# A graph network's edge MLP on one core: the layer-1 bias, a node-row split and an update bias change engines

## The chip, the core and the metric

The kernel runs on one core of one Trainium2 chip. The core has five engines, each with a queue of its own that is worked off strictly in order: TensorE (PE, with its weight loads shown apart as PEld), VectorE (DVE), ScalarE (ACT), GpSimd (POOL) and SyncE (SP, which here issues all the DMAs of the steady part). [...]The metric is the device time of the whole kernel in microseconds (us), lower is better.

## What is computed

128 graphs of 64 nodes with 128 channels. Every pair (i, j) of a graph goes through a two-hidden-layer MLP, the messages are masked by the adjacency and summed over j, and a second MLP updates the nodes:

```
def _mlp(x, w0, b0, g0, be0, w1, b1, g1, be1, w2, b2):
    h = relu(x @ w0 + b0);  h = _layernorm(h, g0, be0)
    h = relu(h @ w1 + b1);  h = _layernorm(h, g1, be1)
    return h @ w2 + b2

messages = _mlp(concat(x_i, x_j)) * adj[..., None]
agg      = sum(messages, axis=2)
out      = x + _mlp(concat(x, agg))
```

Everything is float32. About one pair in eight is an edge, so the kernel works on edges only.

## The kernel before

**Tiles.** Two graphs make a pair; a graph has 640 edge slots (CAP). Four graphs make a "quad" of 20 tiles of 128 edges, worked in **5 chunks (QC) of 4 tiles (CH)**: 160 chunks in all (NCHK). Four pairs make a block, so a block is 10 chunks, and there are 16 blocks.

**Algebra that matters here.** The first layernorm is not applied to the hidden layer; its weights are centred beforehand (`w1c`), and its scale is taken out of the ReLU. What is left of it is that the layer-1 bias `b1b` must be multiplied by each edge's standard deviation before it is added: z = h·w1c + sd·b1b, then y = relu(z). sd·b1b is what the code calls the *seed*. It is a 128 x 512 tile per chunk.

**The order is written out by hand.** The whole edge path is one loop over steps n (L1035). In step n, in this order: the plan's places "a" and "m"; layer 1 of chunk n-8 (`layer1`, L609); place "b"; layer 0 of chunk n (`layer0`, L553); the transposes and first statistics of chunk n-1 (`stats0`, L574); place "k"; the second statistics of chunk n-8 (`stats1`, L619); and the places "x", "x1", "x2", "e0", "e1", "e". `at(n, place, fn)` puts a piece of work into the plan. This order fixes the order in each engine's queue; no scheduler changes it. Steps repeat every 10 (a block), so "step 3" below means n = 3 modulo 10.

**What one chunk does.**
- `layer0`: the 512 edge columns of a chunk come from up to two graphs (`pieces`, L544: one piece of 512, or 128+384, 256+256, 384+128); each piece takes two matmuls, one with the low and one with the high part of the node rows (`abl`, `abh`), into the single PSUM bank `hps`; ScalarE adds the bias and clamps (L562).
- `stats0`: four transposes into the single bank `hT`; VectorE takes statistics from there (L261).
- `seed` (L595): writes sd·b1b into one of two PSUM banks `z` (bank n % 2). For the chunks chosen by `by_vector` (L879: 3, 4 and 8 of ten, more at start and end) VectorE writes it with one instruction (L601), for the rest ScalarE with four (L606). It is planned two steps ahead of the matmuls (place "x").
- `layer1`: four matmuls (eight passes in the trace) accumulate on the seed already lying in the bank, with start=False; ScalarE clamps to `y` (L617). [...]`prime` (L591) runs one dummy matmul into each z bank at the beginning.
- `stats1`: VectorE takes statistics of `y`. Later GpSimd makes the weights `w` (L650) and TensorE sums edges into nodes (`reduce`, L653).

**What one block does besides.** `rows` (L467) projects the nodes of four graphs into a PSUM bank, twice a block (steps 8 and 3); `rows_hi` (L479) rounds them to `abh` with ScalarE and `rows_lo` (L489) makes `abl`, the rest, with VectorE, both one step later, reading the bank. `make_tp` (L504) makes slot masks on VectorE, `node_rows` (L512) casts them on GpSimd, `compare` (L537) makes the second half on VectorE; SP carries both into `S`. `place` and `place_out` (L398, L411) make the positions `posall` on GpSimd, which the `marks` matmuls read from step 5 on. The update MLP of the block runs stretched over sixteen steps (L812 to L845): its first bias `m0` = deg·c2u + ub0b is made by `bias0` (L696) with four VectorE instructions at step 3, the residual `xo` (L705) and the bias product `usdb` (L748) by GpSimd.

`add_relu` (L243) is one custom VectorE instruction that adds a PSUM tile and an SBUF tile and clamps at zero; before the change only the update MLP uses it (L245). `ubank` and `abank` (L320, L324) are two single PSUM banks for all this side work.

Of the kernel before, what the change touches and what calls it, by code (L numbers as in the profile page):

```python
# [9 lines left out]
F32 = mybir.dt.float32  # L10
# [3 lines left out]
AF = mybir.ActivationFunctionType  # L14
ALU = mybir.AluOpType
# [9 lines left out]
def tile_gnn(  # L25
# [40 lines left out]
    nc = tc.nc  # L66
    B, N, C = x.shape
    P = 128
# [8 lines left out]
    CH = 4  # L77
    QC = QT // CH
    NCHK = NQ * QC
    PB = 4  # L80
    NB = NP // PB
    CPB = NCHK // NB
# [23 lines left out]
    blkp = ctx.enter_context(tc.tile_pool(name="blk", bufs=3))  # L106
# [54 lines left out]
    cmpt = const.tile([P, CAP], F16, name="cmpt")  # L161
# [3 lines left out]
    slot = const.tile([P, CAP], F16, name="slot")  # L165
# [9 lines left out]
    W = {}  # L175
# [62 lines left out]
    def bc(t, n, axis=1):  # L238

        s = [P, n, C] if axis == 1 else [P, C, n]  # L240
        return t.unsqueeze(axis).to_broadcast(s)

    def add_relu(o, ps, sb):  # L243

        nc.vector._custom_dve(TENSOR_ADD_SAT, out=o, in0=ps, in1=sb, s0=BIG, s1=0.0)  # L245
# [56 lines left out]
    def edge_path(es):  # L302
# [2 lines left out]
        sp = es.enter_context(tc.tile_pool(name="sp", bufs=4))  # L305
        hp = es.enter_context(tc.tile_pool(name="hp", bufs=9))
        yp = es.enter_context(tc.tile_pool(name="yp", bufs=15))
        lp = es.enter_context(tc.tile_pool(name="lp", bufs=3))
        wp = es.enter_context(tc.tile_pool(name="wp", bufs=2))
        updp = es.enter_context(tc.tile_pool(name="upd", bufs=1))  # L310
        stp = es.enter_context(tc.tile_pool(name="stp", bufs=5))
# [8 lines left out]
        def abank():  # L320

            return ps_a.tile([P, 512], F32, name="ma")

        def ubank():  # L324

            return ps_u.tile([P, 512], F32, name="mu")
# [13 lines left out]
        def at(n, place, fn, *args):  # L340
            plan.setdefault((n, place), []).append((fn, args))

        def run(n, place):
            for fn, args in plan.pop((n, place), ()):
                fn(*args)

        blocks = {b: {} for b in range(NB)}
        TP, S, H, ST0, V0, Y, ST1, Q, OH, WT, YS, MK, D, IR, JR, SR, Z = ({} for _ in range(17))


        def load_adj(b):
# [115 lines left out]
        def rows(b, half, k0=0, k1=4):  # L467

            blk = blocks[b]
            ps = blk["ab_ps", half] if k0 else abank() if (b, half) == (0, 1) else ubank()  # L470
            for k in range(k0, k1):
                s = slice((4 * half + k) * N, (4 * half + k + 1) * N)
                nc.tensor.matmul(ps[0:N, k * C:(k + 1) * C], lhsT=blk["xnT"][:, s], rhs=w0a,
                                 start=True, stop=True)
                nc.tensor.matmul(ps[N:P, k * C:(k + 1) * C], lhsT=blk["xnT"][:, s], rhs=w0b,
                                 start=True, stop=True)
            blk["ab_ps", half] = ps

        def rows_hi(b, half, k0=0, k1=4):  # L479

            blk = blocks[b]
            if k0 == 0:
                blk["ab", half] = [blkp.tile([P, 4, C], F32R, name=v, bufs=2)
                                   for v in ("abl", "abh")]
            hi = blk["ab", half][1]
            ps = blk["ab_ps", half].rearrange("p (k c) -> p k c", k=4)
            nc.scalar.copy(hi[:, k0:k1], ps[:, k0:k1])  # L487

        def rows_lo(b, half, k0=0, k1=4):  # L489
            blk = blocks[b]  # L490
            lo, hi = blk["ab", half]
            ps = blk["ab_ps", half].rearrange("p (k c) -> p k c", k=4)
            nc.vector.tensor_tensor(lo[:, k0:k1], ps[:, k0:k1], hi[:, k0:k1].bitcast(F32),  # L493
                                    op=ALU.subtract)
            if k1 == 4:
                del blk["ab_ps", half]
# [47 lines left out]
        def pieces(n):  # L544

            at_, end = n * CH * P, (n + 1) * CH * P
            while at_ < end:
                g, e = divmod(at_, CAP)
                w = min(end - at_, CAP - e)
                yield g, e, at_ - n * CH * P, w  # L550
                at_ += w

        def layer0(n):  # L553

            ps = ps_h.tile([P, CH * P], F32, name="hps")
            for g, e, c, w in pieces(n):
                s = S[g // 2][:, g % 2, e:e + w]
                for k, ab in enumerate(blocks[g // (2 * PB)]["ab", g // 4 % 2]):
                    nc.tensor.matmul(ps[:, c:c + w], lhsT=ab[:, g % 4, :], rhs=s,  # L559
                                     start=(k == 0), stop=(k == 1))  # L560
            H[n] = hp.tile([P, CH * P], F32, name="h")
            nc.scalar.activation(H[n], ps, AF.Relu, bias=b0c)  # L562
# [22 lines left out]
        def z_of(n):  # L585

            if n not in Z:
                Z[n] = zbank(n % 2).rearrange("p (t c) -> p t c", t=CH)
            return Z[n]

        def prime(n):  # L591
            nc.tensor.matmul(z_of(n), lhsT=slot[:, 0:P], rhs=cmpt[:, 0:CH * C], start=True,
                             stop=True, skip_group_check=True)

        def seed(n):  # L595

            q, c = divmod(n, QC)
            z = z_of(n)
            k = CH * c
            if by_vector(n):  # L600
                nc.vector.tensor_tensor(  # L601
                    z, bc(W["b1b"], CH),
                    SR[q][:, k:k + CH].unsqueeze(2).to_broadcast([P, CH, C]), op=ALU.mult)
                return
            for t in range(CH):
                nc.scalar.activation(z[:, t, :], W["b1b"], AF.Copy,  # L606
                                     scale=SR[q][:, k + t:k + t + 1])

        def layer1(n):  # L609

            ps = Z.pop(n)
            h = H.pop(n)
            for t in range(CH):
                nc.tensor.matmul(ps[:, t, :], lhsT=h[:, t * P:(t + 1) * P], rhs=W["w1c"],  # L614
                                 start=False, stop=True, skip_group_check=True)
            Y[n] = yp.tile([P, CH, C], F32, name="y")
            nc.scalar.activation(Y[n], ps, AF.Relu)  # L617

        def stats1(n):  # L619
            q, c = divmod(n, QC)  # L620
# [74 lines left out]

        def bias0(u):  # L696
            u.m0 = wide("m0", u)
            for q in range(u.n):
                nc.vector.scalar_tensor_tensor(
                    u.m0[:, q, :], W["c2u"], u.blk["deg"][:, u.k0 + q:u.k0 + q + 1], W["ub0b"],  # L700
                    op0=ALU.mult, op1=ALU.add)

        def residual(u):
            u.xo = wide("xo", u)
# [73 lines left out]
        L1 = QC + 3  # L778
# [8 lines left out]
        for b in range(NB):  # L787
            o = b * CPB
            if b > 1:
                at(max(o - 19, 0), "a", load_adj, b)  # L790
                at(max(o - 12, 0), "a", load_x, b)
            if b > 0:
                r = max(o - 12, 1)
                at(max(o - 14, 0), "m", rank, b)
                at(r, "x", count, b)
                at(r + 1, "a", count_out, b)
                at(r + 1, "a", degrees, b)
                at(max(o - 9, r + 1), "e", place, b)
                at(*((r + 2, "a") if b == 1 else (o - 7, "e")), place_out, b)
                at(max(o - 7, 13), "m", odd_weights, b)  # L800
                at(o - 3, "x", turn_x, b)
                at(o - 2, "a", turn_x_out, b)
            for half, n in ((0, o - 2), (1, o + 3)):
                if n >= 0:
                    at(n, "x2", rows, b, half)
                    at(n + 1, "a", rows_hi, b, half)
                    at(n + 1, "m", rows_lo, b, half)
        for b in reversed(range(NB)):
            o = b * CPB
            n = o + QC + SC  # L810

            if b < NB - 1:  # L812
                t = STEADY if b < NB - 3 else LAST[b - NB + 3]
# [65 lines left out]
        def by_vector(n):  # L879
            if n >= NCHK - L1:  # L880
                return n % 2 == 1
            return n % CPB in (3, 4, 8) or (n < CPB and n % CPB in (1, 5))

        for n in range(2):
            at(L1 - 1 - n, "s", prime, n)
            at(L1 - 1, "x", seed, n)
        for n in range(2, NCHK):
            at(n + L1 - 2, "x", seed, n)

        warm = ps_y.tile([P, PB, C], F32, name="ys")  # L890

# [143 lines left out]
        for n in range(last + 1):  # L1035
            run(n, "a")
            run(n, "m")
            if n == NCHK:
                stats0(n - 1)
            run(n, "s")  # L1040
            if 0 <= n - L1 < NCHK:
                layer1(n - L1)
            run(n, "b")
            if n + LEAD < QC or QC <= n < NCHK:
                layer0(n if n >= QC else n + LEAD)
            if n + 1 < QC or QC <= n - 1 < NCHK - 1:
                stats0(n - 1 if n > QC else n + 1)
            run(n, "k")
            if 0 <= n - L1 < NCHK:
                stats1(n - L1)  # L1050
            for k in ("x", "x1", "x2", "e0", "e1", "e"):
                run(n, k)
# [166 lines left out]
```

## Time and profile before

| | us |
|---|---|
| three runs of the kernel | 544.13, 546.4 (median), 2212.09 |
| the profiled execution | 544.21 |
| its span, first to last instruction | 542.4 |
| GpSimd busy in it | 207.4 (38%) |
| granted TensorE clock, mean | 0.996 |

The third run is far from the other two and is left aside. The span is split into a start (the first layer-1 matmul comes at 34.5 us), a steady part, and an end without new chunks. In the steady part ten chunks take 31.15 to 31.19 us, read from the start of one chunk's layer-1 matmuls to that of the chunk ten later. In views of groups a row gives source line, engine, operation, output and inputs, shape and count; then busy time and mean duration; then the idle time just ahead of these instructions and what ended it. TensorE's busy time is modelled from overlapping matmuls, so a full PE row doesn't say that it never waits.

### The profile page before, as it was taken

To read this page: it belongs to the slowest core of one execution; us is meant where nothing else is said; L and a number is where in the kernel's file an instruction comes from. 1 tells how busy PE (TensorE), PEld (TensorE's weight loads), DVE (VectorE), ACT (ScalarE), POOL (GpSimd) and SP (SyncE) were. 2 spreads that over 40 slices of the span, in tenths; PEclk is the share of its full clock that TensorE was granted. 3 is DMA by queue.
4 is the path that set the end of the run, shared out by engine and by line. 5 is a ranking of instruction groups with operands and counts; after the bars stand their busy time and mean duration, and the time that the engine had idled before them with its cause. 6 is when DMAs were issued, how large, how long until landed. Compare 5 with 4: busy or idle time off the path is not lost. (4 is left out here: it accounts for less than half of the span.)

```text
span 542.4 us, 15157 instructions
## 1 busy us (share of the span) xinstructions
PE 520.0 (96%) x5513; PEld 471.6 (87%) x5513; DVE 472.3 (87%) x1271; ACT 475.0 (88%) x1108; POOL 207.4 (38%) x419
## 2 busy tenths in 40 slices
PE   8989999999999999999999999999999999999784
PEld 7777889899898989989898989989999998988764
DVE  6759798998989899898989989898989989896745
ACT  6788999998989999898999989899999989887824
POOL 3103253525334363533435353443536254323230
PEclk9999999999999999999999999999999999999998
DMA  4456666545575665547464554557466445542101
GB/s 99 106 134 117 154 110 149 124 115 121 121 164 101 154 109 128 130 101 166 113 148 96 148 136 98 145 122 147 103 149 129 119 110 117 142 99 32 39 22 43
DMA packets 90762, 63.18 MB, mean 116 GB/s; under 512 B 57398, under 2 KB 74812, under 8 KB 90684
## 3 DMA queue, kind: packets, MB, share of 16 engines
q1 hardware_dynamic: 90396, 62.03, 51.3%
q8 instruction: 46, 0.75, 0.6%
q14 instruction: 32, 0.26, 0.1%
q10 hardware_dynamic: 288, 0.13, 0.1%
HBM read 6.82 MB, written 4.19 MB: 20 GB/s over the span
## 5 line engine op out<-in xcount | busy, mean ns | idle before, releaser
L614 PE MATMUL z<-w1c,h 128*128 128x128 f32 x1280 | 175.8, 280 | 5.2 <-DVE z L601 2.5
L614 PEld LDWEIGHTS z<-w1c,h 128*128 128x128 f32 x1280 | 155.6, 191 | 18.8 <-DVE z L601 8.6
L606 ACT ACTIVATE z<-b1b,m_sd 128x128 f32<-128x128 f32 x436 | 162.1, 372 | 10.7
L261 DVE BATCH_NORM_STATS2 st<-hT 128x6 f32<-128x256 f32 x320 | 118.8, 412 | 20.5 <-PE hT L568 18.3
L261 DVE BATCH_NORM_STATS2 st<-y 128x6 f32<-128x256 f32 x320 | 120.7, 418 | 4.2 <-ACT y L617 4.2
L617 ACT ACTIVATE y<-z 128x512 f32<-128x512 f32 x160 | 94.8, 593 | 20.6 <-PE z L614 19.1
L562 ACT ACTIVATE h<-hps,b0c 128x512 f32<-128x512 f32 x160 | 109.6, 685 | 3.2 <-PE hps L559 3.2
L568 PE MATMUL hT<-ident,h 128*128 128x128 f32 x640 | 97.5, 275 | 2.4 <-DVE st L261 1.3
L559 PE MATMUL hps<-s,abl 128*128 128x512 f32 (+3 forms) x256 | 91.9, 371 | 0.5 <-ACT s L926 0.4
L568 PEld LDWEIGHTS hT<-ident,h 128*128 128x128 f32 x640 | 73.7, 141 | 19.4 <-PE z L614 7.7
L650 POOL TENSOR_TENSOR w<-oh,m_q 128x192 f32<-128x192 f16 x126 | 61.5, 510 | 59.9 <-PE ma L711 25.9
L559 PE MATMUL hps<-s,abh 128*128 128x512 f32 (+3 forms) x256 | 78.0, 323 | 0.0
L517 POOL CAST i<-tp 128x640 fp32r<-128x640 f16 x58 | 41.7, 719 | 93.3 <-issue 47.9
L541 DVE TENSOR_TENSOR j<-mk,cmpt 128x320 fp32r<-128x320 f32 x124 | 58.5, 472 | 1.0 <-PE mk L533 1.0
L502 ACT ACTIVATE d<-slot,mid 128x640 f16<-128x640 f16 x64 | 52.8, 825 | 0.0
L559 PEld LDWEIGHTS hps<-s,abl 128*128 128x128 f32 x256 | 48.9, 191 | 3.6 <-ACT w2cT L200 2.0
L559 PEld LDWEIGHTS hps<-s,abh 128*128 128x128 f32 x256 | 48.9, 191 | 0.1
L665 PE MATMUL ys<-y,w 128*32 128x128 f32 x1488 | 47.0, 275 | 0.0
L665 PEld LDWEIGHTS ys<-y,w 128*32 128x32 f32 x1488 | 38.7, 110 | 4.1 <-issue 3.3
L493 DVE TENSOR_TENSOR abl<-mu,abh 128x512 fp32r<-128x512 f32 (+1 forms) x32 | 21.3, 664 | 22.9 <-ACT abh L487 22.9
L533 PE MATMUL mk<-tp,posall 128*128 128x320 f16 x126 | 37.7, 299 | 0.0
L279 POOL TENSOR_TENSOR m_v<-m_v,st 128x20 f32<-128x20 f32 x31 | 7.7, 250 | 78.3 <-DVE st L261 74.7
(204 smaller groups left out, 841.9 us busy)
## 6 DMA issues: line engine op xcount, KB each, us to landing
s<-i SPq DMA_DIRECT2D x124, 160.0 KB, 2.9
s<-j SPq DMA_DIRECT2D x124, 160.0 KB, 2.7
xn<-in_x_dram SPq DMA_DIRECT2D x15, 256.0 KB, 3.6
out_dram<-uo SPq DMA_DIRECT2D x15, 256.0 KB, 2.9
an<-in_adj_dram SPq DMA_DIRECT2D x16, 128.0 KB, 2.5
oh<-tp SPq DMA_TRANSPOSE x64, 3.3
xn<-in_x_dram SPq DMA_DIRECT2D x2, 128.0 KB
out_dram<-uo SPq DMA_DIRECT2D x2, 128.0 KB, 3.0
```

Source lines behind the costliest of these rows:

```text
L261: nc.vector.bn_stats(st, src.rearrange("p t c -> p c t"))
L502: nc.scalar.activation(D[p], slot, AF.Abs, bias=blocks[b]["mid"][:, q:q + 1], scale=-1.0)
L517: nc.gpsimd.tensor_copy(IR[p], TP[p])
L541: nc.vector.tensor_tensor(JR[p][:, c], MK.pop((p, k))[:, 0:HC], cmpt[:, c], op=ALU.is_equal)
L559: nc.tensor.matmul(ps[:, c:c + w], lhsT=ab[:, g % 4, :], rhs=s, start=(k == 0), stop=(k == 1))
L562: nc.scalar.activation(H[n], ps, AF.Relu, bias=b0c)
L568: nc.tensor.transpose(ps[:, t, :], H[n][:, t * P:(t + 1) * P], ident)
L606: nc.scalar.activation(z[:, t, :], W["b1b"], AF.Copy, scale=SR[q][:, k + t:k + t + 1])
L614: nc.tensor.matmul(ps[:, t, :], lhsT=h[:, t * P:(t + 1) * P], rhs=W["w1c"], start=False, stop=True, skip_group_check=True)
L617: nc.scalar.activation(Y[n], ps, AF.Relu)
L650: (nc.vector if p == NP - 2 else nc.gpsimd).tensor_tensor(WT[p][:, g], oh, qs, op=ALU.mult)
L665: nc.tensor.matmul(YS[b][g * N + m * HN:g * N + (m + 1) * HN, k, :], lhsT=w[:, g, m, u, :], rhs=y, start=(u == 0), stop=(u == TH - 1), til ...
```

## The change

`seed` without tiles now means: GpSimd writes sd·b1b into an SBUF tile `u` (pool `up`, three buffers; it takes the place of an unused pool). `by_vector` picks chunks 1 and 3 of five. For those, layer 1 starts its bank itself (start=True on the first matmul) and VectorE's `add_relu` adds `u` and clamps, in place of the ScalarE clamp. The other chunks are seeded by ScalarE as before, the first of the four tiles ahead of layer 0's clamp (new place "y"), the other three after it. The priming matmuls are gone. The `rows` of all blocks but the first come one step earlier (steps 7 and 2, the turning of x with them); ScalarE copies them out of PSUM as a float32 tile `ab`, and GpSimd makes the rounded and the low part from that. The first half's rows take the other side bank. `bias0` becomes two GpSimd instructions. `layer0` takes a chunk's wider piece first.

```
-        lp = es.enter_context(tc.tile_pool(name="lp", bufs=3))
+        up = es.enter_context(tc.tile_pool(name="up", bufs=3))
@@ rows
-            ps = blk["ab_ps", half] if k0 else abank() if (b, half) == (0, 1) else ubank()
+            ps = blk["ab_ps", half] if k0 else abank() if (half == 0) == (b > 0) else ubank()
@@ rows_hi
+            if b:
+                ab = blk["ab32", half] = blkp.tile([P, 4, C], F32, name="ab", bufs=2)
+                nc.scalar.copy(ab, ps)
+                del blk["ab_ps", half]
+                return
@@ rows_lo
+            if b:
+                ab = blk.pop(("ab32", half))
+                nc.gpsimd.tensor_copy(hi, ab)
+                nc.gpsimd.tensor_tensor(lo, ab, hi.bitcast(F32), op=ALU.subtract)
+                return
@@ layer0
-            for g, e, c, w in pieces(n):
+            for g, e, c, w in sorted(pieces(n), key=lambda v: -v[3]):
@@ seed
-        def prime(n):
-            nc.tensor.matmul(z_of(n), lhsT=slot[:, 0:P], rhs=cmpt[:, 0:CH * C], start=True,
-                             stop=True, skip_group_check=True)
-
-        def seed(n):
+        def seed(n, *tiles):
             q, c = divmod(n, QC)
-            z = z_of(n)
             k = CH * c
-            if by_vector(n):
-                nc.vector.tensor_tensor(
-                    z, bc(W["b1b"], CH),
+            if not tiles:
+                U[n] = up.tile([P, CH, C], F32, name="u")
+                nc.gpsimd.tensor_tensor(
+                    U[n], bc(W["b1b"], CH),
                     SR[q][:, k:k + CH].unsqueeze(2).to_broadcast([P, CH, C]), op=ALU.mult)
-                return
-            for t in range(CH):
-                nc.scalar.activation(z[:, t, :], W["b1b"], AF.Copy,
+            for t in tiles:
+                nc.scalar.activation(z_of(n)[:, t, :], W["b1b"], AF.Copy,
                                      scale=SR[q][:, k + t:k + t + 1])
@@ layer1
-            ps = Z.pop(n)
+            ps = z_of(n)
+            del Z[n]
+            added = n in U
-                                 start=False, stop=True, skip_group_check=True)
+                                 start=added and t == 0, stop=True, skip_group_check=True)
-            nc.scalar.activation(Y[n], ps, AF.Relu)
+            if added:
+                add_relu(Y[n], ps, U.pop(n))
+            else:
+                nc.scalar.activation(Y[n], ps, AF.Relu)
@@ bias0
-            for q in range(u.n):
-                nc.vector.scalar_tensor_tensor(
-                    u.m0[:, q, :], W["c2u"], u.blk["deg"][:, u.k0 + q:u.k0 + q + 1], W["ub0b"],
-                    op0=ALU.mult, op1=ALU.add)
+            deg = u.blk["deg"][:, u.q].unsqueeze(2).to_broadcast([P, u.n, C])
+            nc.gpsimd.tensor_tensor(u.m0, bc(W["c2u"], u.n), deg, op=ALU.mult)
+            nc.gpsimd.tensor_tensor(u.m0, u.m0, bc(W["ub0b"], u.n), op=ALU.add)
@@ the plan
-                at(o - 3, "x", turn_x, b)
-                at(o - 2, "a", turn_x_out, b)
-            for half, n in ((0, o - 2), (1, o + 3)):
+                at(o - 4, "x", turn_x, b)
+                at(o - 3, "a", turn_x_out, b)
+            for half, n in ((0, o - 3 if b else -1), (1, o + 2 if b else 3)):
@@ by_vector and the seeds' steps
-            return n % CPB in (3, 4, 8) or (n < CPB and n % CPB in (1, 5))
-        for n in range(2):
-            at(L1 - 1 - n, "s", prime, n)
-            at(L1 - 1, "x", seed, n)
-        for n in range(2, NCHK):
-            at(n + L1 - 2, "x", seed, n)
+            return n % QC in (1, 3) or n == 0
+        for n in range(NCHK):
+            if by_vector(n):
+                at(max(n + L1 - 3, L1 - 2), "e0", seed, n)
+            else:
+                at(n + L1 - 2, "y", seed, n, 0)
+                at(n + L1 - 2, "x", seed, n, 1, 2, 3)
@@ the loop over steps
             run(n, "b")
+            run(n, "y")
```

(In the last eight chunks `by_vector` takes every odd one, before and after.)

More of the change, by code (lines that the diff above doesn't have):

```diff
@@ L347, in edge_path @@
         blocks = {b: {} for b in range(NB)}
-        TP, S, H, ST0, V0, Y, ST1, Q, OH, WT, YS, MK, D, IR, JR, SR, Z = ({} for _ in range(17))
+        TP, S, H, ST0, V0, Y, ST1, Q, OH, WT, YS, MK, D, IR, JR, SR, Z, U = ({} for _ in range(18))
         def load_adj(b):
```

## The prediction

> **What bounds the kernel now.** First the busy table, then the same over the steady stretch of 13 blocks (72 to 477 us).
>
> ```profile
> PE 520.0 (96%) x5513; PEld 471.6 (87%) x5513; DVE 472.3 (87%) x1271; ACT 475.0 (88%) x1108; POOL 207.4 (38%) x419
> ```
> ```profile
> 72.00:477.00 405.00, 404.13 (x4394) 370.19 (x4391) 375.00 (x998) 376.25 (x873) 175.46 (x338) 1.00 0.56 126
> ```
>
> The columns are the stretch, its length, then busy time of PE, weight loads, DVE, ACT and POOL. Three engines are nearly full: weight loads 91%, DVE and ACT 93% each; POOL 43%. PE's 100% doesn't tell whether it waits, so next the list of waits for the weight-load queue (where TensorE's waits show) and for VectorE, same stretch: total us, times, longest.
>
> ```profile
> PEld hT L568 <- PE z L614: 7.5, 23, 0.4
> PEld z L614 <- DVE z L601: 5.9, 26, 0.5
> ...
> PEld z L614 <- ACT z L606: 2.2, 13, 0.2
> PEld hT L568 <- PE hps L559: 1.7, 8, 0.5
> ```
> ```profile
> DVE abl L493 <- ACT abh L487: 19.9, 13, 1.7
> DVE st L261 <- PE hT L568: 6.9, 14, 0.6
> ```
>
> TensorE waits 8.1 us for seeds and 9.2 us at the transposes. The latter are put down to matmuls long done; what they really need is the single bank hT, freed by VectorE's statistics. So **VectorE, late, holds up TensorE**. VectorE's idle time is mostly forced: 19.9 of its 30 us it stands at abl until ScalarE has rounded the rows, with other work queued behind. 375 busy and 19.9 forced make 395 of 405. Then the timeline of one step 3 (layer 1 starts at 260.29):
>
> ```profile
> 261.93 0.63 PE L568 MATMUL hT<-ident,h 128*128 128x128 f32 x4
> ...
> 263.22 1.54 POOL L416 TENSOR_TENSOR posall<-pos,an 64x256 f16<-64x256 f32 x2
> ...
> 263.54 1.89 DVE L699 SCALAR_TENSOR_TENSOR m<-c2u,deg,ub0b 128x128 f32<-128x128 f32 x4
> ...
> 265.36 0.75 DVE L261 BATCH_NORM_STATS2 st<-hT 128x6 f32<-128x256 f32 x2
> ...
> 269.41 0.30 PE L533 MATMUL mk<-tp,posall 128*128 128x320 f16 x1
> ```
>
> The transposes of 261.93 are read only at 265.36, 3.4 us later, as bias0 stands ahead.
>
> **What the Trainium skill says.** "Trainium Kernel Development and Optimization", Performance Expectations, calls matmul busy time a bad measure and weight-load busy a good one; the trace agrees (100% beside 17 us of waits). "SBUF — State Buffer", Who interferes with whom: a VectorE instruction in a two-port mode, or with two SBUF inputs against a reading GpSimd, locks out GpSimd or is locked out, for the whole instruction. The trace agrees:
>
> ```profile
> L508 DVE TENSOR_SCALAR tp<-d,deg x53: 347/375/1112, 72.5 to 475.4; 128x640 f16<-128x640 f16 x53
> ```
>
> These are shortest, median and longest in ns: the same slot mask takes 0.36 us free, and up to 1.11 where a product of GpSimd runs beside it. "GPSIMD Engine Reference", Elementwise — side-by-side cycle accounting: 4497 ns for a two-input add of 2048, an estimate of 1.12 us for 512; the trace has 1.04 and 1.29.
>
> **The change, part by part.** Prices: whole-kernel rows.
>
> - *ScalarE*: 436 seed pieces become 376, -60 x 0.372 = -22.3; 66 clamps go, 66 x 0.593 = -39.1. Sum -61 of 475.
> - *VectorE*: 51 seeds go, 51 x 0.682 = -34.8; 30 abl, -20.4; 64 bias0 pieces, -28.1; 66 add_relu come, at 0.673 (the update MLP's, same shape), +44.4. Sum -38.9, and the 19.9 us of forced standing goes too. Against it: L508 averages 0.519 where 0.36 is free, so about 10 us of locking now; with GpSimd nearly twice as busy I add 8 (0 to 15).
> - *GpSimd*: 66 u at 1.042 (usdb, the same broadcast product) = 69; 30 casts, 0.719 x 512/640 = 0.575, 17; 30 subtractions, no such row, between 1.04 and 1.29, I take xo's 1.29, 39; bias0 in two instructions, 15 x (1.04+1.29) = 35, and 3 for the half units. Sum +163: 207 becomes 370, 70% of 530. None of this is on the path as long as its queue keeps its place.
> - *TensorE*: a 128-wide piece first costs 0.086 us between low and high part (seen at abl to abh; absent where the 384 piece leads). 32 chunks, -2.7. Two priming matmuls go, ahead of which PE stood 2.3 us in the start; probably half is waited elsewhere: -1 (0 to -2.3).
> - *Moved steps*: rows leave steps 8 and 3, which have the reduction, for 7 and 2. The same matmuls and ScalarE copies: 0, and as the two fullest steps get 1 us shorter, a small gain isn't excluded (0 to -3). Abl is now ready about 3.1 us into step 3 and wanted by layer 0 in step 5, 7 us in: covered. If GpSimd were 4 us late, layer 0 would wait.
> - *SP*: its DMA instructions keep their order. The casts i may be issued up to one step later behind u; the slots are wanted four steps after the cast, landing takes 2.9: 0; else DMAs queued behind would slip with it.
>
> *New waits.* (1) add_relu waits for layer 1 of its own step; behind it stand the statistics that free hT. VectorE now runs 2 to 3 us late, so layer 1 is done by then; if it is punctual, it idles in time it has: 0. (2) In steps 1 and 6 ScalarE's first seed piece reuses the bank of an added chunk and waits for add_relu; behind it stands layer 0's clamp, which frees hps. From layer 1's start: add ends at 0.9+0.7, piece and clamp end at 2.6, next layer 0 at about 4.0: VectorE may be 1.4 us late at no cost; 0, at worst 0.5 x 26 = 13. (3) Step 3 of GpSimd becomes long, and the positions posall come last in it: cast, subtraction, two bias0, u, two small ones, posall: 0.58+1.29+1.04+1.29+1.04+0.54+1.46 = 7.2, with gaps 7.5. It begins at about 1.2 (after um_v, which waits VectorE), earlier if VectorE is: posall ends 8.2 to 8.7 into the step. The marks want it at 269.41-260.29 = 9.1, less 1.0 for the rows gone from step 3 and 0.2 of waits: 7.9. I take 0.3 us a block, +4 over 13 (0 to 0.9, so 0 to 12).
>
> *Sum, in the steady part.* Seed waits 8.1: added chunks have none, ScalarE is at 79%; -6.5. Transpose waits 9.2: VectorE is lighter, though locked out more; -4.5 (-2 to -9). After a wait the second layer-1 pass starts 0.1 us late, 52 times, 5.4 in all, and goes in proportion, -3.8. Order of pieces -2.7. Marks +4. Start -1; the end, where chunks are few, 0 (+-2). Together -14.5: 544.2 - 14.5 = **530**, against the profiled execution, which equals the lower run (544.13) and lies 0.4% under the median 546.4. The floor is 8.1+9.2+5.4+2.7+2.3 = 28 less: 516.
>
> **Rivals.** *The gain is eaten* (0.20): marks wait 0.9 a block (+12), half of the transposes' wait stays through locking: -14.5+8+2 is about 540. For it: GpSimd's long step 3; against: only one of ten steps is that full. *Nothing is there to gain* (0.08): PE at its floor, waits only move; 542 to 546. For it: PE 100% busy; against: listed waits and the forced stand. *GpSimd becomes the bound, slower* (0.12): its queue needs 370/16 = 23 us per block, and now idles 17.7 (31.16 less 175.46/13), much of it for others in queue order, the largest being
>
> ```profile
> POOL m_v L279 <- DVE st L261: 66.5, 26, 4.3
> ...
> POOL usdb L748 <- DMA s<-j: 25.9, 7, 3.8
> POOL usdb L748 <- ACT um_sd L269: 21.4, 6, 3.8
> ```
>
> With those for ma, m_q and uy (19.1, 18.3, 10.6) that is 162 in 13 blocks, 12 each. A fuller queue comes later to what it waits for, so they shrink; if more than 9 of the 12 stayed, a block would take over 32 us, which is the 2%. At 10 it is 33, 1.9 x 13 = 25 more: 569. u, abl, i and posall would all come late, and TensorE wait for them. Against: the weights and small steps are wanted a step or more after they are queued.
>
> **How the numbers follow.** Main case 0.60, 521 to 535, at 530. 2% is 11 us, about what can be told from no change, so faster means below 535. Faster 0.60; within 0.20 + 0.08 = 0.28; slower 0.12. The range runs from 521 (all but 5 of the floor's gain) to 548 (rivals one and two and their spread); left out are the GpSimd case and little below. The main case's own range is 521 to 535.
>
> **What would show it.** In the profile after: ten chunks take 29.9 to 30.4 us rather than 31.16; waits of layer 1 for seeds are under 2 us and VectorE's stand at abl is gone; L508's mean rises towards 0.65; GpSimd is at 65 to 75%; a wait of the posall load for GpSimd of 0 to 0.9 a block. If posall or abl head the weight loads' waits with over 10 us, the first rival holds; if GpSimd is over 85%, the third. Wrong altogether, if VectorE's lag at hT stays at 3 us though its queue is lighter.

## The result and the profile after

The changed kernel takes **551.05 us** (median, 550.15 to 552.05) against 545.33 before (median, 544.13 to 546.40): a ratio of 1.0106, interval 1.0071 to 1.0142, slower by 1%. Two runs far above all others, 2212.09 us of the kernel before and 1289.96 us of e10 below, are left aside. The forecast was 530. The profiled execution took 550.58 us beside 544.21, +6.4. Ten chunks in the regular stretch take 31.84 us, where it was 31.17 (mean of ten blocks, from the start of layer 1 of chunk 30 to that of chunk 130).

The busy table of the page first, then the steady stretch (72 to 480 us; columns as before).

```profile
PE 518.0 (94%) x5511; PEld 471.7 (86%) x5511; DVE 448.0 (82%) x1192; ACT 423.7 (77%) x982; POOL 361.9 (66%) x579
```
```profile
72.00:480.00 408.00, 396.08 (x4338) 364.11 (x4339) 347.27 (x918) 329.11 (x755) 297.35 (x465) 1.00 0.55 124
```

VectorE fell from 472 to 448 us and ScalarE from 475 to 424. Both falls, 24 and 51, are smaller than the 31 (38.9 less 8 of locking) and 61 that were priced: the durations added up did fall by 38.5 and 65.5, but busy time counts overlapping instructions once. No engine is fuller than before except GpSimd, at 66%. The other engines are idler and the kernel is slower: a wait has come in. From the list of waits of the same stretch:

```profile
...
DVE st L261 <- PE hT L578: 28.5, 52, 1.3
...
PEld L543 <- POOL posall L416: 14.3, 13, 1.2
ACT z L611 <- DVE y L245: 13.3, 18, 2.0
PE mk L543 <- POOL posall L416: 11.3, 13, 0.9
...
PEld mu L734 <- ACT uhT L725: 3.0, 12, 0.3
```

The waits of layer 1 for seeds are gone from the list, and so is VectorE's stand at abl; VectorE now waits for the transposes (28.5 us), not they for it. TensorE's one long wait comes once in every block: the marks of step 5 wait for posall. GpSimd's timeline of one step 3 (layer 1 starts at 264.54) shows why:

```profile
265.89 0.60 POOL L499 CAST abh<-ab 128x512 fp32r<-128x512 f32 x1
266.57 1.28 POOL L500 TENSOR_TENSOR abl<-ab,abh 128x512 fp32r<-128x512 f32 x1
267.81 1.04 POOL L709 TENSOR_TENSOR m<-c2u,deg 128x512 f32<-128x512 f32 x1
268.93 1.28 POOL L710 TENSOR_TENSOR m<-m,ub0b 128x512 f32<-128x512 f32 x1
270.16 1.13 POOL L607 TENSOR_TENSOR u<-b1b,m_sd 128x512 f32<-128x512 f32 x1
271.26 0.26 POOL L278 TENSOR_SCALAR m_v<-st 128x20 f32<-128x20 f32 x1
271.61 0.23 POOL L279 TENSOR_TENSOR m_v<-m_v,st 128x20 f32<-128x20 f32 x1
271.80 1.52 POOL L416 TENSOR_TENSOR posall<-pos,an 64x256 f16<-64x256 f32 x2
```
```profile
273.38 0.31 PE L543 MATMUL mk<-tp,posall 128*128 128x320 f16 x1 [0.89 <-POOL posall L416]
```

Eight steps without a gap take 7.4 us, posall last; TensorE stands at the marks for it. Before, posall ended at 264.76 in such a step and the marks came at 269.41.

Where the 0.68 us of a block go can be read from TensorE alone. Sorting the gaps from each matmul's start to the next one's by the two kinds of matmul, the change of their sums per block is:

| gap | us per block |
|---|---|
| transposes to marks (the wait for posall) | +1.05 |
| layer 0 to its pieces and to the transposes | -0.49 |
| layer 1 behind the turns of uh and uy (the seeds' waits) | -0.28 |
| into the rows' 64-column matmuls, from another neighbour | +0.19 |
| around the update's second layer (ScalarE's copy uhT comes late) | +0.21 |

The start (up to layer 1 of chunk 20) gave +1.0 us, the thirteen blocks from there to chunk 150 +7.3, as the first of them grew by only 0.42 and the last shrank by 0.57, and the end -1.9.

### The profile page after: what moved, and what is told of

Its sections match the earlier page's. It is cut to its first block, busy times and chain, and to the rows that moved or that the text cites. A ratio compares the mean times of both kernels' runs of the same rounds, so it can differ in the third digit from the quotient of the medians.

```text
span 548.8 us, 15143 instructions
## 1 busy us (share of the span) xinstructions
PE 518.0 (94%) x5511; PEld 471.7 (86%) x5511; DVE 448.0 (82%) x1192; ACT 423.7 (77%) x982; POOL 361.9 (66%) x579
## 5 line engine op out<-in xcount | busy, mean ns | idle before, releaser
L611 ACT ACTIVATE z<-b1b,m_sd 128x128 f32<-128x128 f32 x376 | 138.7, 369 | 28.3 <-DVE y L245 18.9
L261 DVE BATCH_NORM_STATS2 st<-hT 128x6 f32<-128x256 f32 x320 | 121.1, 420 | 39.4 <-PE hT L578 37.2
L572 ACT ACTIVATE h<-hps,b0c 128x512 f32<-128x512 f32 x160 | 108.0, 675 | 24.8 <-PE hps L569 24.7
L607 POOL TENSOR_TENSOR u<-b1b,m_sd 128x512 f32<-128x512 f32 x66 | 70.2, 1065 | 62.8 <-ACT m_sd L269 62.8
L569 PE MATMUL hps<-s,abh 128*128 128x512 f32 (+3 forms) x256 | 74.6, 323 | 0.0
L660 POOL TENSOR_TENSOR w<-oh,m_q 128x192 f32<-128x192 f16 x126 | 62.6, 509 | 9.9 <-PE hps L569 5.2
L627 ACT ACTIVATE y<-z 128x512 f32<-128x512 f32 x94 | 55.2, 587 | 10.7 <-PE z L621 10.7
L499 POOL CAST abh<-ab 128x512 fp32r<-128x512 f32 x30 | 18.7, 622 | 66.4 <-ACT ab L489 66.3
L245 DVE CUSTOM_DVE_ANT_0 y<-z,u 128x512 f32<-128x512 f32 x66 | 45.1, 684 | 15.8 <-PE z L621 15.0
```

What stands on the lines that cost most here:

```text
L261: nc.vector.bn_stats(st, src.rearrange("p t c -> p c t"))
L607: nc.gpsimd.tensor_tensor(U[n], bc(W["b1b"], CH), SR[q][:, k:k + CH].unsqueeze(2).to_broadcast([P, CH, C]), op=ALU.mult)
L611: nc.scalar.activation(z_of(n)[:, t, :], W["b1b"], AF.Copy, scale=SR[q][:, k + t:k + t + 1])
L660: (nc.vector if p == NP - 2 else nc.gpsimd).tensor_tensor(WT[p][:, g], oh, qs, op=ALU.mult)
```

## The experiments

All were timed against the kernel before on the same chip; they ran on four chips, so runs are compared by their ratio or their time per block. "Block" is ten chunks, as above. Lines with "after" start from the changed kernel; the text gives the start of the others. Shares of a block are sums of gaps between matmuls, taken as above over chunks 30 to 130 of each trace.

| run | us | ratio to before, interval | us per block |
|---|---|---|---|
| before, changed | 545.33, 551.05 | 1.0071 to 1.0142 | 31.17, 31.84 |
| e1 after, posall a step earlier | 562.41 | 1.0319 to 1.0367 | 32.64 |
| e2 rows' steps alone | 545.05 | 0.9999 to 1.0032 | 31.16 |
| e3 wider piece first alone | 543.83 | 0.9980 to 1.0011 | 31.13 |
| e4 after, rows' part undone | 540.98 | 0.9922 to 0.9960 | 30.92 |
| e8 after, bias0 a step later | 545.08 | 0.9978 to 1.0019 | 31.30 |
| e6 after, bias0 undone | 551.61 | 1.0115 to 1.0166 | 31.80 |
| e10 seeds' part alone | 564.43 | 1.0350 to 1.0405 | 32.76 |
| e7 bias0 on GpSimd alone | 539.51 | 0.9888 to 0.9952 | 30.75 |
| e12 after, bias0 later, turning of x later | 540.34 | 0.9875 to 0.9946 | 30.88 |
| e13 bias0 and wider piece | 539.07 | 0.9870 to 0.9926 | 30.73 |
| e14 as e12, seeds of before | 539.80 | 0.9886 to 0.9941 | 30.84 |
| e15 as e13, abl behind the slot mask | 536.03 | 0.9798 to 0.9860 | 30.47 |

**e1: move posall out of the long step.**

```
-  at(*((r + 2, "a") if b == 1 else (o - 7, "e")), place_out, b)
+  at(*((r + 2, "a") if b == 1 else (o - 8, "e")), place_out, b)
```

> The changed kernel with the positions posall made one step earlier on GpSimd (step 2 in place of step 3, ahead of the row split, the update bias and u). Theory A, posall stands last in GpSimd's long step 3 and TensorE's marks wait about 1.0 us a block for it: that wait is gone, ten chunks take 30.8 us in place of 31.84, the kernel 535 to 539 us against 551 for the changed kernel. Rival B, GpSimd's queue as a whole is late: the 1.5 us that posall takes is only handed on to abl, u or the weights, layer 0 or layer 1 wait instead, 546 to 551.

The marks' wait went exactly (-1.05 a block), and yet the kernel lost 11 us more. Rival B was right that the time is only handed on, but named other receivers and too small a loss. ScalarE's timeline and GpSimd's, steps 4 and 5 of one block:

```profile
274.99 0.83 ACT L512 ACTIVATE d<-slot,mid 128x640 f16<-128x640 f16 x1
277.05 0.31 ACT L285 ACTIVATE m_sq<-m_v,eps_c 128x20 f32<-128x20 f32 x1 [1.23 <-POOL m_v L279]
277.27 0.58 ACT L627 ACTIVATE y<-z 128x512 f32<-128x512 f32 x1
...
278.19 0.67 ACT L572 ACTIVATE h<-hps,b0c 128x512 f32<-128x512 f32 x1
```
```profile
275.44 1.03 POOL L607 TENSOR_TENSOR u<-b1b,m_sd 128x512 f32<-128x512 f32 x1
276.44 0.26 POOL L278 TENSOR_SCALAR m_v<-st 128x20 f32<-128x20 f32 x1
276.79 0.23 POOL L279 TENSOR_TENSOR m_v<-m_v,st 128x20 f32<-128x20 f32 x1
```

The 1.6 us of posall push the small m_v back. ScalarE's root of it (L285) heads step 5, and behind it stand the clamp of y and the clamp of layer 0, which frees hps. Layer 0 of step 6 waits 1.34 us a block for that, and the turning of x, of which e8 below tells, another 0.42. So step 3's GpSimd queue has two deadlines, and shortening the way to one lengthens the way to the other. What must shrink is the queue.

**e8: take bias0 (2.3 us) out of that step, into the empty step 4.**

```
-  units = [(Unit(b, 0, PB, nc.gpsimd, ubank), n, t, 0, t[5] - 1)]
+  units = [(Unit(b, 0, PB, nc.gpsimd, ubank), n, t, 1, t[5] - 1)]
```

> The changed kernel with the update bias bias0 one step later (step 4, where GpSimd has nothing else queued; it is wanted in step 7). Theory A, what the change lost is GpSimd's overfull step 3 alone: posall and the variance m_v end 2.3 us earlier, neither the marks nor ScalarE's root wait, a block loses the 1.05 us of the marks' wait: 30.7 us per ten chunks, 533 to 537. Rival B, something behind it holds as well (as with posall moved earlier, where m_v became the next): the cast of step 5, w or u come late and TensorE waits at layer 0 or the reduction, 543 to 552.

The marks' wait went (-1.05) and no root waits; but only 0.54 a block came through: rival B's range, though the place is none that it named. The head of TensorE's list of waits shows the next one:

```profile
PEld z L621 <- issue: 9.6, 52, 0.2
PEld ma L459 <- ACT uyT L725: 6.1, 12, 0.5
PEld mu L473 <- issue: 3.3, 14, 0.2
PEld mu L734 <- ACT uhT L725: 3.2, 13, 0.3
```

The turning of the next block's x, moved to step 6 with the rows, needs the side bank ma, which ScalarE is still emptying of uyT: 0.42 us a block. In the changed kernel TensorE's stand at the marks in step 5 had hidden it.

**e12: e8, and the turning of x behind the update's first layer in step 6.**

```
-  at(o - 4, "x", turn_x, b)
+  at(o - 4, "x1", turn_x, b)
```

> The changed kernel with bias0 in step 4 and, in step 6, the turning of the next block's x after the update MLP's first layer in TensorE's queue (place x1 in place of x). Theory A, what held bias0-later at 545 is the single side bank ma: moved to step 6, the turning of x waits there 0.42 us a block for ScalarE to copy uyT out, while 0.9 us of matmuls stand behind it that don't need the bank; with those ahead the wait is covered: 30.9 us per ten chunks, 537 to 540. Rival B, TensorE is then full and gains nothing, or the next of VectorE's or ScalarE's waits takes its place: 543 to 546.

30.88 us a block, 540.34: theory A, at the edge of its range. The marks' wait is gone, and so is the one for ma that its going had laid bare; together that is 0.97 us a block off the changed kernel, and it now beats the kernel before by 0.9%.

**e2, e3: two parts alone.** e2 takes the plan's lines for turn_x and rows and the bank rule from the change, e3 the `sorted` in layer0.

> The kernel before with the rows (and the turning of x, and the side bank of the first half) one step earlier, all on the engines of before. Theory A, the rows' 64-column matmuls cost TensorE about 0.2 us at each change of matmul shape, and away from the reduction there are two such changes more a block: 0.2 to 0.4 us a block, 548 to 552 against 545.5. Rival B, the step matters by VectorE: rows away from the full steps end its stand at abl, 538 to 543.

> The kernel before with only layer 0's wider piece first. Theory A, TensorE is the bound and the 0.086 us gap after a 128-wide low part is pure loss in 2 of 10 chunks: 0.2 us a block, 542 to 543.5 against 545.5. Rival B, VectorE's lateness sets the pace and TensorE only waits longer at the transposes: 545 to 546.

Neither moves the time, and neither falls into the range of one of its theories. In e2 gains and losses cancel: the matmuls into 64 columns and the layer 1 behind them lose 0.3 a block, the turning of x 0.37, while waits for VectorE shrink by 0.6. In e3 only two of ten chunks change their order (128 and 384 columns become 384 and 128). In each, the time from the 128-wide low part to its high part falls from 0.143 to 0.059 us, as expected; but the same time of the 384-wide piece rises from 0.229 to 0.262 and the three between transposes by 0.025 together, so that 0.025 us a chunk is left. And step 3, whose order is unchanged, loses 0.04 at its transposes.

**e4: undo the rows' part. e6: undo bias0. e10, e7: seeds alone, bias0 alone.**

> The changed kernel with the whole row part undone (steps 8 and 3, banks of before, abl on VectorE from PSUM, no ab copy). Theory A, posall's place and the rows' step are what the change lost: GpSimd's step 3 is 1.9 us shorter, marks wait under 0.2 us a block, the two extra changes of matmul shape are gone, 533 to 538. Rival B, VectorE's stand at abl was what bounded the kernel before: it returns with 1 to 1.5 us a block, TensorE waits at the transposes again, 541 to 546.

> The changed kernel with bias0 back on VectorE (four instructions at step 3). Theory A as above: GpSimd's step 3 is 2.3 us shorter, the marks' wait is gone, 533 to 539, if VectorE can carry 1.9 us at step 3 without its rows. Rival B, VectorE at step 3 is what counts: statistics of hT come 1.9 us late, TensorE waits at the transposes in step 4 or ScalarE's first seed piece waits for add_relu: 541 to 548.

> The kernel before with the seeds' part alone: u by GpSimd and add_relu on VectorE for two chunks of five, no priming, the first seed piece ahead of layer 0's clamp; rows, bias0 and the order of pieces as before. Theory A, TensorE is all but full, and the seeds hold only about 0.3 to 0.5 us a block: 538 to 542 against 544.5. Rival B, VectorE was the bound: it keeps its rows and bias0 and gets 0.67 in place of 0.68 us, four times a block in place of three, so it is later than before: 546 to 556.

> The kernel before with bias0 alone on GpSimd (two instructions at step 3, ahead of m_v and posall). Theory A, GpSimd has the room here (posall ended 4.6 us before the marks) and TensorE is all but full: 542 to 545 against 544.5. Rival B, VectorE was the bound and is freed of 1.9 us at its worst step: 530 to 538.

e4 lies just below its rival B: the marks' wait is gone, but VectorE's stand at abl is back (20.0 us) and the transposes behind a 512 piece cost 0.58 a block more than in the changed kernel. e6 lost the marks' wait and got 0.87 a block at the transposes of steps 4 and 5 instead: VectorE can't carry bias0 at step 3 beside add_relu. One of its four pieces takes 0.82 us there on average, and took 0.53 in the kernel before. e10, where VectorE keeps its rows too, is worse: seeds alone cost 3.8%. Both e6 and e10 are slower than either of their theories had it. The steady stretch of e10 and its timeline around step 4:

```profile
72.00:480.00 408.00, 384.67 (x4198) 351.39 (x4197) 388.98 (x969) 319.54 (x735) 217.25 (x377) 1.00 0.55 121
```
```profile
261.28 0.69 DVE L493 TENSOR_TENSOR abl<-mu,abh 128x512 fp32r<-128x512 f32 x1 [1.43 <-ACT abh L487]
261.89 1.11 DVE L508 TENSOR_SCALAR tp<-d,deg 128x640 f16<-128x640 f16 x1
262.01 0.60 PE L568 MATMUL hT<-ident,h 128*128 128x128 f32 x4
262.92 0.68 DVE L245 CUSTOM_DVE_ANT_0 y<-z,u 128x512 f32<-128x512 f32 x1
...
263.52 0.75 DVE L261 BATCH_NORM_STATS2 st<-hT 128x6 f32<-128x256 f32 x2
...
264.42 0.63 PE L568 MATMUL hT<-ident,h 128*128 128x128 f32 x4 [0.44 <-DVE st L261]
```

VectorE is at 95%. Abl, the mask and add_relu stand ahead of the statistics; before, the seed was written behind them, with two steps to spare. The transposes wait 1.9 us a block more. An add_relu costs VectorE the same 0.68 us as the seed it replaces, but at a place where the statistics stand behind it. The place is not the whole of it: VectorE's busy time rises by about 2.4 us a block, 0.7 of it for the fourth add_relu, and 1.7 because other instructions take longer beside a busier GpSimd. In the steady stretch the mask's mean goes from 0.54 to 0.71 us, the first product of the odd weights (L451) from 0.41 to 1.08, a piece of bias0 from 0.53 to 0.61. No run separates the two causes.

e7 is the best of the four: 1.9 us off VectorE at its worst step give 0.42 a block, 539.51, faster than either kernel. That lies between its two theories. Of the 0.42, 0.16 comes at the transposes, 0.14 at a seed that is now in time and 0.10 in the layer 1 behind it.

**e13, e14, e15: from there.** e13 is e7 with `sorted`; e14 is e12 with the seeds of before; e15 is e13 with one place changed:

```
-  at(n + 1, "m", rows_lo, b, half)
+  at(n + 1, "b", rows_lo, b, half)
```

> The kernel before with two parts of the change: bias0 on GpSimd and the wider piece first. Theory A, alone the order of pieces gave nothing because the transposes behind it waited for VectorE anyway (0.27 us a block more there); with VectorE relieved at step 3 its 0.17 to 0.35 us a block come through: 30.5 us per ten chunks, 534 to 537.5. Rival B, VectorE sets the pace still: as bias0 alone, 539 to 540.

> As bias-later-turn-x-late, but with the seeds of before (VectorE and ScalarE write them into PSUM; no u, no add_relu). It tells what the seeds' part is worth once VectorE has neither rows nor bias0. Theory A, seeds are not what TensorE waits for then, and add_relu only brings VectorE into the step's own chain: this is as fast as with u or faster, 535 to 540. Rival B, ScalarE at 93% is the next bound and the u were needed: 542 to 547, with waits of layer 1 for ScalarE's seeds and of hps for ScalarE's clamp.

> As the kernel with bias0 on GpSimd and the wider piece first, and abl one place later in VectorE's queue (place b in place of m), so that a slot mask stands ahead of it instead of behind it while VectorE stands waiting for the rounded rows 1.6 us a block. Theory A, VectorE's stand is still what makes the remaining waits: by the smallest gap of each kind seen in any run, TensorE could do ten chunks in 30.2 us, and 0.1 to 0.3 us of the 0.5 left come through: 30.45 to 30.65, 535 to 538 us. Rival B, the mask is not what was late: 538 to 540, no difference; or abl comes too late for layer 0 of the next step, which waits for VectorE: 540 to 545.

e13 equals e7, and its two reordered chunks again gain only 0.025 us each: so it wasn't VectorE's lateness that kept e3 from gaining. (Of the 0.27 us in theory A 0.22 is no wait: it is the gaps of two more 128-wide pieces, which now stand ahead of the transposes where two 384-wide ones stood.) e14 equals e12: the seeds' part saves 0.24 us a block at a late seed, and pays 0.22 for a late copy of uhT and 0.08 at layer 0, so it gains nothing once bias0 and the rows have left VectorE. e15 gains 0.26 a block over e13, nearly all at one layer 1 that waited for VectorE's seed. It is the fastest, 536.03, **1.7% under the kernel before** (interval 1.4 to 2.0) and 15 us under the changed one. What is left of TensorE's waits for seeds and at the transposes in it:

```profile
...
PEld hT L568 <- PE hps L559: 2.5, 13, 0.2
PEld z L614 <- issue: 2.4, 14, 0.2
PEld z L614 <- ACT z L606: 2.2, 13, 0.2
...
PEld z L614 <- DVE z L601: 0.5, 1, 0.5
```

Seeds 2.7 and transposes 2.5, where before it was 8.1 and 9.4 in this stretch.

## Why the prediction was wrong, step by step

The forecast sum for 13 blocks beside what a block's gaps give, times 13:

| term | forecast | measured |
|---|---|---|
| seeds' waits | -6.5 | -3.6 |
| transposes' waits | -4.5 | -5.7 |
| restarts of layer 1 | -3.8 | 0 |
| order of the pieces | -2.7 | -0.8 |
| marks wait for posall | +4 | +13.7 |
| rows' moved steps | 0 (0 to -3) | +2.4 |
| uhT late | none | +2.7 |
| start and end | -1 | -0.9 |

(The order of the pieces is what the two reordered chunks of a block gained in the changed kernel; the transposes' share is the rest of that line of the gaps, with the gaps between transposes. Thirteen regular blocks would be +8.8, where the stretch gave +7.3; so the table gives +7.8 for the +6.4.)

- **The step that turned the sign is new wait (3), the marks.** Its mechanism was named and its prices held: 7.4 us for the eight steps, forecast 7.5; u 1.07, subtraction 1.28, cast 0.62. What was mis-sized is what remains: posall ending 8.2 to 8.7 into the step and wanted at 7.9, from which 0.3 was taken with 0.9 at most. It ended 8.8 in, was wanted at 7.7 and cost 1.05. e8 and e1 show that it is this wait: moving bias0 or posall takes exactly 1.05 away. Two estimates of over 7 us were subtracted, and the low end of a difference as small as their error was used.
- **The step that made the expected gain too large is the floor.** 17.3 us of idle weight-load queue, 5.4 of restarts and 2.7 of order were added up as TensorE's loss. The gaps between matmuls show less. The 26 waits for VectorE's seed (5.9 us, 0.23 each) delayed the matmuls by 0.14 each, 3.6 in all. The 13 put down to ScalarE's seed (2.2 us) stand behind the rows, where layer 1 starts just as late (0.20) in the changed kernel, with no seed to wait for. At the transposes about 5.7 us were lost, not 9.2. Of the four late restarts of a block two stand behind the rows and not behind a seed; the moved rows and the reduction make two new ones where the seeds' two go, so nothing was gained there. An estimate of the floor: with the smallest mean gap for each pair of matmuls seen in before, e7 and e10, the order of before needs 30.24 us a block, so 0.92 x 13 = 12 us were to be had, not 25.4. For the order after, its own variants (changed, e1, e6, e8, e12) need 30.75, or 30.54 with e14, where uhT is in time: the moved order takes about 0.3 of the 0.92 away before anything waits.
- Moved steps at "0, or a small gain": wrong. Separated from the reduction, the rows cost 0.19 a block, and their turning of x meets a bank still in use (0.42, hidden until e8 removed what covered it). ScalarE's late copy uhT (0.21) comes in all five kernels with both the rows' and the seeds' part (changed, e1, e6, e8, e12), and in none of those with one of the two (e2, e4, e10, e14). In the changed kernel it stands behind three pieces of a seed in ScalarE's queue (1.17 us); more is not shown.
- Order of the pieces: the gap is real, but the reordered chunk gives back most of what its removal saves (e3, e13: 0.025 us of 0.084 is left).
- Reading VectorE as late and holding TensorE up: right. e7 and e15 change VectorE's queue at single places and gain 0.42 and 0.26 a block.
- New waits (1) and (2), add_relu in the step's own chain and ScalarE's seed behind it: both came (13.3 us on ScalarE) and cost the changed kernel next to nothing (0.8 us at layer 0), as forecast. e10, where VectorE is late and ScalarE waits 36.6 us for add_relu, shows that this holds only while VectorE is punctual.
- Locking: the mask's mean was to rise from 0.519 towards 0.65. It is 0.530, with GpSimd at 66% in place of 38%. The rule of the Trainium skill ("SBUF — State Buffer", Who interferes with whom) isn't contradicted: one mask in each block still takes 1.0 to 1.1 us. The count of such meetings just didn't grow with GpSimd's load in this kernel. It depends on what runs beside what, as e10 shows, where nearly two masks a block are slow, with GpSimd busy for 53% of the steady stretch (73% in the changed kernel).
- Rivals: the first (the gain is eaten at the marks) is what happened; its 540 was too low, by the overestimated floor. GpSimd as the bound is not: at 66% it stands waiting for ab for 53.5 us of the stretch, and is late only in step 3.

## What to carry to other kernels

An engine at 66% can still be the one that is late: add up its queue in the fullest step and hold every deadline of that step against it, not its share of the span. Work moved off a crowded engine should be put where the receiving queue is empty (bias0 one step later was worth 6 us). After mending one wait, look for the next that it had hidden. And price a possible gain by the gaps between matmuls, not by idle time of the weight loads.

## What the runs showed of the hardware

- Changing between matmuls of 128 columns and of 64 or 32 cost TensorE time at each change. Rows and the reduction started 0.229 us after marks, other matmuls 0.136; rows started 0.205 after the update's layer. From the reduction to rows, from the reduction to layer 1, and from rows to layer 1 it was 0.20 us, where layer 1 started 0.11 to 0.14 behind others that held nothing up. So rows between the reduction and layer 1 add one such change, and rows elsewhere two: the moved rows cost 0.19 us a block.
- A layer 1 that started late, behind such a change or behind a late seed, had its second pass 0.21 us after the first instead of 0.11.
- A 128-wide low part at the head of layer 0 took 0.143 us to its high part, and 0.059 behind a 384-wide piece. The whole chunk, from layer 1 through its transposes, gained only 0.025 us by the other order (1.017 to 0.991 us at step 6).
- The same VectorE instruction took 0.41 us (L451, before) and 1.08 us (e10, with u on GpSimd beside it).
